# A graph network on one core: the opening of the kernel rebuilt

## The chip, the cores and the metric

The kernel runs on one core of one Trainium2 chip. A core has a matrix engine (TensorE, PE in the profile; its weight loads are PEld), a vector engine (VectorE, DVE), an activation engine (ScalarE, ACT), a general engine (GpSimd, POOL) and an engine that only issues transfers (SyncE, SP). Each engine works through its own list of instructions in order and waits for semaphores of the others. Transfers (DMA) are issued from SP, ACT or POOL and share 16 DMA engines. The metric is device time in microseconds (us) of one execution.

## What is computed

One layer on 64 graphs of 256 nodes with 256 features. The input is normalised per node and clipped at zero. Then come a convolution branch of width 1 and then 17 along the nodes, a message branch over an affinity matrix (with the given adjacency as a mask), and a gated recurrent unit that joins both; its result is added to the input.

```python
h = jnp.maximum(_layernorm(x, axis=-1), 0.0)
# inside the layer, on h:
h1 = relu(bn1(conv1(h)));  h2 = bn2(conv2(h1))       # conv2 has 17 taps, pad 8
x_conv = relu(h2 + h)
s = h @ w_se.T + b_se                                  # 3 features
A = exp(-dist(s)) * adj
x_nmp = A @ relu(h @ w_msg.T + b_msg)
gi = concat(x_conv, x_nmp) @ w_ih.T + b_ih
gh = h @ w_hh.T + b_hh
r, z = sigmoid(gi_r + gh_r), sigmoid(gi_z + gh_z)
out = x + (1 - z) * tanh(gi_n + r * gh_n) + z * h
```

All of it is float32.

## The kernel before

**Work and tiles.** Two graphs make a pair (`i`), four pairs a batch (`b`); there are 32 pairs and eight batches. The wide convolution is done in a transformed domain: each stretch of 16 nodes is transformed to 16 bins (`forward`, on DVE: `fft.odd` gives what bins 0 to 7 need, `fft.even` bins 8 to 15), every bin is multiplied with a transformed filter (`product`, on PE), and the products are transformed back (`branch_back`, `odd_back`, `q_back`, `p_back`, `join`, on DVE). Of each complex bin three real products are made, "kinds" 0, 1 and 2; bin 15 has two. That makes 47 products per batch, in the order of the list `TURNS`. `begin(m)` makes kind 0 of bins 2m and 2m+1, `complete(m)` the other kinds and evicts the result to `Yv` (odd bins) or `Yu`. Each product needs one transformed filter of 256 KB in one of nine slots `wb`, loaded by SP from the DRAM tensors `filt` (`load_kinds`), two new ones after each product that frees a slot.

**The opening.** The transformed filters are made once, at the start. The 17 taps of seven input channels are one group (`KG`); there are 18 full groups and a last one. `filters(p, m, g, eng)` multiplies group `g` of `taps` with the points of pass `m` (two matmuls of 256 columns), ACT evicts the result into one of eight buffers `fo` (the ring `evicted`), and a DMA from SP or POOL, in turn, stores it to `filt[m]`. Before, pass 0 has the bins 0 to 5, pass 1 the bins 6 to 11, pass 2 the bins 12 to 15, so 18, 18 and 11 columns per channel. The order is in `steps`: all passes of the first six groups, pass 0 of the others, the last group, then passes 1 and 2 of the others. `filter_steps(n)` plans the next `n`. The taps are loaded in three parts per half (`dc`), half 0 by SP and half 1 by ACT (lines 703 to 713).

Meanwhile the first four pairs are loaded, normalised (`stats`, `norm`: `bn_stats` and `bn_aggr` on DVE, a power on POOL for `rstd`, then the normalising on DVE), transposed on PE (`transpose_h`), passed through the first convolution (`conv1`, evicted with bn1's scale and shift) and combined into U and V (`split`). PE runs 35 matmuls on zeros first (`WARM`). The batch-norm vectors are loaded by POOL as rows and turned into columns by a transpose on PE (`columns`, `fold_bn`). Lines 1260 to 1293 are the opening: pairs with filter steps between them, `forward(0)` and `forward(1)`, filter steps, `load_kinds()`, `message(0)`, eight steps, `embed(0)`, four steps, `affinity(0)`, the remaining steps. `message` makes the messages and the 3-feature embedding, `embed` transposes the embedding, `affinity` makes exp(-dist) and masks it with the adjacency; `aggregate` multiplies with the messages.

**What sets the order.** The code above does not run as written. Every call goes through a `Recorder`, which notes for each instruction what it reads and writes. `emit()` then plans all instructions noted since the last `emit()`: it simulates the five engines and two DMA queues with estimated costs (line 334 on), and gives each engine, whenever it is free, the ready instruction with the earliest due time. Due times follow from the written order of PE's instructions. Instructions recorded while `nc.first` is set (the loads, the memsets before line 714) come first of all; `nc.behind = k` makes those that follow wait in the plan for instruction `k`. At most eight DMAs are planned in flight for SP and ACT together, eight for POOL. Before, the first `emit()` comes after the last filter step (line 1292), and the second, for all the rest, at the end. Tiles that only the opening needs (`taps`, `fo`, `points`) are in a pool that is closed there, and `Yv`, `w_x` and others take its place.

All recorded instructions carry line 371 in the profile; they are told apart by their tiles.

## Time and profile before

| | us |
|---|---|
| median of 6 runs | 1710.48 |
| lowest and highest run | 1705.96, 1714.1 |
| time of the profiled execution | 1705.96 |
| its span, first to last instruction | 1704.2 |
| PE busy in the span | 1667.5 |
| DVE busy | 1464.9 |
| ACT busy | 1043.0 |
| first matmul that is no warm-up | at 11.37 |
| first product | at 90.7 |

Times in the profile count from the start of the span. A row of the timeline gives start, length, engine, line, operation, the tiles written and read (`out<-in`), partitions and elements, how many instructions are merged in it, and in brackets the idle time of the engine before it with what ended that. PE busy time holds matmuls that run slowly and warm-ups, so a busy PE is not yet a useful one. The granted clock is a share of TensorE's full rate. Every float32 matmul is two records.

### The profile page before, as it was taken

What the parts mean: (1) busy time and instruction counts of PE and PEld (TensorE: products, weight loads), DVE (VectorE), ACT (ScalarE), POOL (GpSimd) and SP (SyncE); (2) the same over time, 40 slices, a digit from 0 to 9 for tenths busy, and PEclk for the clock granted to TensorE, in tenths of its full rate; (3) what the DMA queues carried; (4) which work ended last, traced back from release to release, by engine and by line L of the source; (5) the groups of instructions that cost most, each with busy time, mean ns of one, the idle gap of its engine ahead of it and who ended that gap; (6) DMA issues with size and microseconds to landing.
All of it is one profiled execution on the core that took longest, in us unless ns stands there. A gap on an engine that the chain in (4) does not pass through costs nothing.

```text
span 1704.2 us, 26232 instructions
## 1 busy us (share of the span) xinstructions
PE 1667.5 (98%) x9012; PEld 1422.0 (83%) x9012; DVE 1464.9 (86%) x3414; ACT 1043.0 (61%) x1951; POOL 222.2 (13%) x245
## 2 busy tenths in 40 slices
PE   8999999999999999999999999999999999999998
PEld 6788888888789788897888887898888978898886
DVE  7969899798897998799987998979988899879645
ACT  3545665577657756576565766567665776557453
POOL 4210021013110121101210021101211012000010
PEclk9999999999999999999999999999999999999999
DMA  9883565976469475783659745694656936484132
GB/s 231 268 266 111 123 129 109 279 161 131 110 170 265 92 139 111 202 237 76 135 113 260 180 90 119 132 288 121 124 114 187 250 90 121 100 240 128 23 61 51
DMA packets 326928, 261.47 MB, mean 153 GB/s; under 512 B 205011, under 2 KB 252399, under 8 KB 326794
## 3 DMA queue, kind: packets, MB, share of 16 engines
q1 hardware_dynamic: 294193, 214.32, 48.2%
q0 software_dynamic: 29520, 42.76, 13.3%
q10 hardware_dynamic: 3081, 2.71, 0.7%
q8 instruction: 71, 1.16, 0.3%
q14 instruction: 63, 0.52, 0.1%
HBM read 156.60 MB, written 43.78 MB: 118 GB/s over the span
## 4 chain that ended last, share of the span: by engine, by line
PE 82%; DVE 11%; DMA 4%; ACT 1%; issue 1%; ACTq 0%; SPq 0%; DVEq 0%
PE acc L371 56%; PE aux L371 26%; DVE V L371 2%; DVE T L371 2%; DMA wb<-filt 2%; DVE Yv L371 1%; DVE U L371 1%; DMA taps<-in_c_wT_dram 1%; DVE gn L371 1%; DVE tr L371 1%; DVE acc L371 1%; DVE wb L371 1%; DMA filt<-fo 1%; DVE msg L371 0%; DVE PT L371 0%
## 5 line engine op out<-in xcount | busy, mean ns | idle before, releaser
L371 PE MATMUL acc<-wb,w_ih 128*128 128x256 f32 x768 | 191.9, 379 | 0.0
L371 PEld LDWEIGHTS acc<-wb,w_ih 128*128 128x128 f32 x768 | 145.9, 190 | 19.8
L371 POOL DMA_DIRECT2D back<-in_x_dram x62 | 62.0, 1158 | 674.0 <-ACT back L371 568.9
L371 PE MATMUL aux<-wb,w_x 128*128 128x256 f32 x576 | 141.6, 383 | 0.6 <-ACT e L371 0.5
L371 DVE SCALAR_TENSOR_TENSOR V<-T,V 128x128 f32<-128x128 f32 (+2 forms) x448 | 141.3, 385 | 0.0
L371 POOL TENSOR_TENSOR rstd<-rstd,neg_half 128x4 f32<-128x4 f32 x32 | 74.7, 2335 | 505.6 <-DVE shift L371 302.8
L371 PE MATMUL acc<-wb,w_x 128*128 128x256 f32 x576 | 136.4, 381 | 1.8 <-DVE acc L371 1.8
L371 PEld LDWEIGHTS acc<-wb,w_x 128*128 128x128 f32 x576 | 108.1, 190 | 28.0 <-DVE acc L371 7.5
L371 PEld LDWEIGHTS aux<-wb,w_x 128*128 128x128 f32 x576 | 107.4, 190 | 20.8 <-issue 4.0
L371 PE MATMUL aux<-w_msg,hT 128*128 128x259 f32 x512 | 120.9, 381 | 0.0
L371 PE MATMUL acc<-V,wb 128*128 128x128 f32 x1024 | 120.4, 278 | 0.1
L371 PEld LDWEIGHTS acc<-V,wb 128*128 128x128 f32 x1024 | 118.2, 194 | 0.7 <-issue 0.3
L371 PEld LDWEIGHTS acc<-U,wb 128*128 128x128 f32 x1024 | 117.3, 192 | 0.9
L371 PE MATMUL acc<-U,wb 128*128 128x128 f32 x1024 | 117.9, 275 | 0.0
L371 PE MATMUL aux<-hT,w_c 128*128 128x512 f32 x224 | 107.9, 596 | 2.9 <-ACT e L371 2.7
L371 PE MATMUL acc<-wb,w_hh 128*128 128x256 f32 x384 | 110.0, 381 | 0.7 <-ACT acc L371 0.7
L371 PE MATMUL acc<-Yv,w_ih 128*128 128x256 f32 x380 | 108.0, 380 | 0.6 <-ACT Yv L371 0.6
L371 PEld LDWEIGHTS aux<-w_msg,hT 128*128 128x128 f32 x512 | 96.5, 190 | 14.4
L371 PE MATMUL acc<-hT,w_hh 128*128 128x256 f32 x380 | 104.5, 382 | 0.0
L371 PE MATMUL acc<-xnm,w_ih 128*128 128x256 f32 x380 | 103.9, 380 | 0.0
L371 PE MATMUL aux<-e,msg 128*128 128x256 f32 x448 | 103.1, 379 | 0.0
L371 ACT COPY back<-gn 128x1024 uint16<-128x1024 uint16 x62 | 80.5, 1351 | 32.3 <-DMA gn<-back 32.3
(190 smaller groups left out, 3787.4 us busy)
## 6 DMA issues: line engine op xcount, KB each, us to landing
wb<-filt SPq DMA_DIRECT2D x376, 256.0 KB
back<-in_x_dram POOLq DMA_DIRECT2D x62, 256.0 KB, 7.4
out_dram<-back POOLq DMA_DIRECT2D x62, 256.0 KB, 4.4
x<-in_x_dram SPq DMA_DIRECT2D x58, 256.0 KB
halves_d<-halves SPq DMA_DIRECT2D x28, 512.0 KB
adjh<-halves_d SPq DMA_DIRECT2D x112, 128.0 KB
hh<-halves SPq DMA_DIRECT2D x108, 128.0 KB
filt<-fo SPq DMA_DIRECT2D x18, 252.0 KB
```

The lines of the kernel that those rows point to most:

```text
L371: self.tasks.append(Task(engine, lambda: method(*args, **kw), cost, size, self.first))
```

## The change

- The loads of the opening are issued by SP: of ACT's there remain the first convolution's weights and the first points. The first points are loaded before x, bn2's vectors later, on POOL, behind the first power. The memsets of `h1` and `Z` are put behind it too.
- `WARM` is 21 instead of 35.
- The second pair's first statistics are planned behind the first pair's `rstd` addition, and its third behind the first pair's normalising. Two blocks of the first pair and all of pairs 1 to 3 are normalised on ACT (scale `rstd`, bias `h`, a new small DVE operation). One half of the first pair's relu and of its conv1 eviction go to ACT. bn1's columns and fold are planned behind the first two matmuls of conv1.
- The passes hold 16, 16 and 15 columns, cut from the list of turns (`PASSES`, `PLACE`), so the rows of `filt` are in the order of use.
- The `fo` buffers are pieces of `Yv`, which now lives from the start; the last pass is evicted onto the taps that it has just used.
- `forward` does the odd part of both halves first, then the even part of both.
- The last twelve filter steps, `embed(0)` and `affinity(0)` are written among `begin` and `complete` of bins 0 to 7, and the first `emit()` comes after `odd_back`.
- The adjacency of pairs 0 to 3 is loaded by `blocks` (rows in their order in memory); the copies in `embed` and `affinity` permute for it.

```diff
@@ passes and tiles
-    WARM = 35
+    WARM = 21
+    Yvt = keep("Yv", SL)
+    Yv = Slots(Yvt, GB * DC, L // 2, NW)
...
-            load_rows(adj_rows, adj, i, eng)
+            load_rows(adj_rows, adj, i, eng, blocks)
...
-    PASSES = [range(0, 6), range(6, 12), range(12, 16)]
+    TURNS = []
+    for m in range(0, BINS // 2, 2):
+        TURNS += [(n, 0) for n in range(2 * m, 2 * m + 4)]
+        for n in range(2 * m, 2 * m + 4, 2):
+            TURNS += [(k, kind) for kind in (1, 2) for k in (n, n + 1) if (k, kind) != (BINS - 1, 2)]
+    PASSES = [TURNS[a:a + 16] for a in range(0, len(TURNS), 16)]
+    PLACE = {t: (m, k) for m, p in enumerate(PASSES) for k, t in enumerate(p)}
-    evicted = Ring(stage.tile([P, W], FP, name=f"fo{k}") for k in range(8))
+    evicted = Ring(Yvt[:, k * W:(k + 1) * W] for k in range(8))
@@ loads
+    nc.scalar.dma_start(out=w_c1, in_=c1_wT.rearrange("(k p) o -> p k o", p=P))
     load_vectors("bn1", bn1, nc.gpsimd)
-    load_vectors("bn2", bn2 + [ih_b, hh_b], nc.gpsimd)
-    nc.scalar.dma_start(out=w_c1, in_=c1_wT.rearrange("(k p) o -> p k o", p=P))
+    load_points(0, nc.scalar)
     for j in range(PB):
         load_x(j)
-    load_points(0, nc.scalar)
-    for dc, eng in ((0, nc.sync), (1, nc.scalar)):
-        load_taps(dc, *PARTS[0], eng)
-        load_last_taps(dc, eng)
+    for dc in range(DC):
+        load_taps(dc, *PARTS[0], nc.sync)
+        load_last_taps(dc, nc.sync)
     for n in range(1, len(PASSES) + 1):
-        load_points(n, nc.scalar)
+        load_points(n, nc.sync)
     for part in PARTS[1:]:
-        load_taps(0, *part, nc.sync)
-        load_taps(1, *part, nc.scalar)
-    load_last_group(0, nc.sync)
-    load_last_group(1, nc.scalar)
+        for dc in range(DC):
+            load_taps(dc, *part, nc.sync)
+    for dc in range(DC):
+        load_last_group(dc, nc.sync)
     nc.first = None
-    nc.gpsimd.memset(Z, 0.0)
...
-    nc.gpsimd.memset(h1, 0.0)
@@ stats, norm
         for j in range(G * MC):
+            nc.behind = BEHIND.get((i, j))
             nc.vector.bn_stats(s[:, j, :], X[i][:, j, :])
+        nc.behind = None
...
         nc.vector.tensor_scalar(r, m[:, :, 1], LN_EPS, None, ALU.add)
+        if i < PB:
+            BEHIND[i + 1, 0] = nc.last["vector"]
...
     def norm(i):
         stats(i)
+        _, m, r, h = STATS[i]
+        if i < PB:
+            nc.vector.scalar_tensor_tensor(h, m[:, :, 0], -1.0, r, op0=ALU.mult, op1=ALU.mult)
         for j in range(G * MC):
-            nc.vector.tensor_scalar(X[i][:, j, :], X[i][:, j, :], STATS[i][1][:, j, 0:1], STATS[i][2][:, j:j + 1],
-                                    ALU.subtract, ALU.mult)
+            v = X[i][:, j, :]
+            if i == PB or (i == 0 and j < MC):
+                nc.vector.tensor_scalar(v, v, m[:, j, 0:1], r[:, j:j + 1], ALU.subtract, ALU.mult)
+            else:
+                nc.scalar.activation(v, v, AF.Identity, scale=r[:, j:j + 1], bias=h[:, j:j + 1])
+        if i == 0:
+            BEHIND[1, MC] = nc.last["vector"]
@@ transpose_h, conv1
-            if i == 0:
+            if i == 0 and dc == 0:
                 nc.vector.tensor_scalar(t, u, 0.0, None, ALU.max)
...
+            if i == o == 0:
+                nc.behind = nc.last["tensor"]
+                bn1 = columns("bn1")
+                nc.behind = None
+                S1.extend(fold_bn(bn1, "bn1"))
...
-            if i == 0:
+            if i == 0 and o == 0:
                 nc.vector.tensor_scalar(v, u, s1[:, o:o + 1], h1_shift[:, o:o + 1], ALU.mult, ALU.add)
@@ filters, load_kinds
-        t = evicted()
+        t = taps[:, g].rearrange("p c o -> p (c o)") if m == len(PASSES) - 1 else evicted()
...
-            m = n // len(PASSES[0])
-            nc.sync.dma_start(out=slots[WB[-1][0]], in_=filt[m][:, 3 * (n - PASSES[m][0]) + kind])
+            m, k = PLACE[n, kind]
+            nc.sync.dma_start(out=slots[WB[-1][0]], in_=filt[m][:, k])
@@ the opening
     norm(0)
-    bn1 = columns("bn1")
-    s1, h1_shift = fold_bn(bn1, "bn1")
+    power = nc.behind = nc.last["gpsimd"]
+    nc.gpsimd.memset(h1, 0.0)
+    nc.gpsimd.memset(Z, 0.0)
...
+    load_vectors("bn2", bn2 + [ih_b, hh_b], nc.gpsimd)
+    nc.behind = None
...
-    forward(0)
-    forward(1)
-    filter_steps(len(steps) - (FULL - FIRST) - 4)
+    for kind in (0, 1):
+        for k in range(2):
+            forward(k, (kind,))
+    THIRD = FULL - FIRST
+    filter_steps(len(steps) - THIRD - 8)
     pending.extend(TURNS)
     load_kinds()
     message(0)
     filter_steps(8)
-    embed(0)
-    filter_steps(4)
-    affinity(0)
-    filter_steps(len(steps))
-    nc.emit()
-    stage_ctx.close()
...
@@ the loop over batches
         complete(0)
-        if b > 0:
-            embed(i)
+        embed(i)
         complete(1)
         fft.branch_back(Yv, T, 0)
+        if b == 0:
+            filter_steps(THIRD // 2, False)
         begin(2)
+        affinity(i)
...
         begin(3)
+        if b == 0:
+            filter_steps(len(steps), False)
         complete(2)
         complete(3)
         if b == 0:
             norm(nxt)
         fft.branch_back(Yv, T, 2)
         fft.odd_back(Yv, T)
+        if b == 0:
+            nc.emit()
+            stage_ctx.close()
...
```

With `wide` false, `filter_steps` takes its PSUM banks from `aux` alone, since the products hold `acc`.

## The prediction

> **What bounds the kernel now.** I read the page first: busy shares, then the chain that ended last.
>
> ```profile
> span 1704.2 us, 26232 instructions
> PE 1667.5 (98%) x9012; PEld 1422.0 (83%) x9012; DVE 1464.9 (86%) x3414; ACT 1043.0 (61%) x1951; POOL 222.2 (13%) x245
> PE 82%; DVE 11%; DMA 4%; ACT 1%; issue 1%; ACTq 0%; SPq 0%; DVEq 0%
> ```
>
> PE is busy for 98% of the span and is 82% of the chain. The change removes no useful matmul (filter evaluation stays at 55 steps of four records), so it can only win time in which PE stands, runs warm-ups or runs slowly. I looked for that time in the PE rows of the timeline from 0 to 170 us (columns: start, length, what, idle before it).
>
> ```profile
> 1.84 9.69 PE L371 MATMUL aux<-e 128*128 128x128 f32 x70 [1.84 <-POOL e L371]
> 11.37 0.27 PE L371 MATMUL aux<-ident,x 128*128 128x128 f32 x1
> 13.55 3.70 PE L371 MATMUL acc<-hT,w_c 128*128 128x512 f32 x8 [0.67 <-DVE hT L371]
> 17.09 0.93 PE L371 MATMUL aux<-ident,T 128*128 128x128 f32 x7
> 19.69 1.10 PE L371 MATMUL aux<-taps,points 119*126 119x256 f32 x4 [1.68 <-DMA taps<-in_c_wT_dram]
> 67.03 1.13 PE L371 MATMUL acc<-taps,points 119*126 119x256 f32 x4 [1.22 <-ACT fo L371]
> 84.75 0.66 PE L371 MATMUL aux<-ident,e 128*128 128x128 f32 x4 [1.10 <-DVE e L371]
> 107.19 0.52 PE L371 MATMUL aux<-ident,z 128*128 128x128 f32 x2 [0.46 <-ACT z L371]
> 108.48 0.69 PE L371 MATMUL aux<-zT 9*128 9x256 f32 x2 [0.77 <-ACT zT L371]
> 109.57 0.69 PE L371 MATMUL aux<-zT 9*128 9x256 f32 x2 [0.39 <-ACT zT L371]
> 162.97 1.13 PE L371 MATMUL acc<-Yv,w_ih 128*128 128x256 f32 x4 [0.59 <-ACT Yv L371]
> ```
>
> Useful work starts at 11.37; after it the waits up to 165 us are 1 to 2 us each. The DVE rows and SP's rows of the same view tell why the start is late:
>
> ```profile
> 9.71 0.43 DVE L371 BATCH_NORM_STATS2 st<-T 128x6 f32<-128x256 f32 x1 [2.19 <-DMA T<-in_x_dram]
> 10.06 1.37 DVE L371 TENSOR_SCALAR x<-x,mv,rstd 128x256 f32<-128x256 f32 x4
> 9.33 10.49 SPq L371 DMA_DIRECT2D taps<-in_c_wT_dram x5
> ```
>
> The first pair's `rstd` was ready at 8.37 (POOL's power, 7.33 plus 1.04), but its normalising stood behind statistics of the second pair, which waited 2.19 for its rows. Last, the table of windows (busy time of PE, PEld, DVE, ACT, POOL; granted clock; DMA share; GB/s):
>
> ```profile
> 0.00:20.00 20.00, 15.68 (x96) 13.02 (x97) 12.55 (x48) 2.08 (x3) 14.09 (x29) 1.00 1.00 212
> 40.00:50.00 10.00, 10.00 (x48) 8.24 (x48) 9.95 (x36) 6.37 (x12) 3.59 (x6) 1.00 0.68 194
> 70.00:80.00 10.00, 10.00 (x49) 7.72 (x48) 9.98 (x33) 7.36 (x20) 2.66 (x5) 1.00 1.01 319
> 111.00:114.00 3.00, 3.00 (x17) 3.00 (x16) 2.89 (x6) 0.27 (x1) 0.00 (x0) 0.51 0.31 87
> 166.00:169.00 3.00, 3.00 (x8) 2.37 (x8) 2.78 (x7) 1.44 (x4) 0.38 (x1) 0.50 0.00 0
> ```
>
> DMA is full at the start and almost full around 75 us. Twice, after PE's waits at 106 to 110 and 162 to 165, the granted clock is halved, for about 3.4 us each: in the trace's records matmuls start 213 ns apart from 111.1 to 114.5 instead of 111, and 427 instead of 216 from 165.7 to 169.1. A spell costs half its length, 1.7.
>
> **The change, part by part** (gains positive).
>
> *First normalising.* The second pair's statistics now stand behind `rstd` and behind the first normalising, and vector loads and memsets on POOL behind the power. The aggregate ends at 6.38 as before; `rstd`'s addition 0.2, hand-over and power 1.25 (the row gives 1.04 plus 0.18 of wait), the shift 0.2: 8.05. Two blocks on DVE at 0.34 end at 8.75; two on ACT at 0.5 apart (the later rows `hh<-x,shift,rstd` last 0.59) end at 9.25. Eight transposes at 0.11 keep PE until 9.9; the first half of hT is evicted on DVE (0.65 per block), the other on ACT (0.60). conv1 starts at 10.4 instead of 13.55: +3.1. The 21 warm-ups end, by the old rows (16 records to 5.34, then 0.11 each for 26), at 8.2, so they hold nothing. bn1's transpose (0.13) and its fold (0.69 on POOL) move behind conv1's first half; DVE needs s1 only after it, at about 14. No cost; uncovered it would be about 1, the fold's chain.
>
> [...] From 8.2 to 10.4 PE would have only 0.9 us of transposes; before, 17.09 to 19.69 held 0.8 us of transposes in 2.6 us and the clock stayed at 1.00, so I take nothing. [...]
>
> *Loads on SyncE.* ACT issued five taps loads and the three later points loads; all go to SP behind the eight x loads. Before the first filter step SP and ACT must bring 256 KB of w_c1, 57 of points, 2048 of x, 2 x 336 and 2 x 126 of taps, 3.28 MB. At the window's 212 GB/s that is 15.5 us: landing at about 16.3 instead of 19.5. PE is ready for it at 10.4 + 3.4 (conv1) + 0.9 (transposes) = 14.7, so the wait is 1.6 against 1.68: +0.1. Bounds: no wait, +1.7; taps landing as late as before, -3.1. SP's remaining loads last until about 25 us; queued behind them are its first filter stores, which had to wait until 22.11 before as well, and eight eviction buffers cover that.
>
> *Norms of pairs 1 to 3 on ACT.* Twelve operations move from DVE (0.34) to ACT (0.5): 6 us more on ACT between 10 and 40 us, where its three windows of 10 us were busy for 0.60, 5.45 and 5.03. hT and h evictions queue behind them, and PE waits for hT. From 0 (ACT has room) to 2 (one 0.5 us block ahead of each of four hT): -0.6, nearer to the free side.
>
> *Filters in thirds of 16, 16, 15 columns, by turn.* A store of the first two thirds shrinks from 252 to 224 KB, of the last grows from 154 to 210. For 24 stores before the products that is 0.67 MB less, 2.4 us of DMA at 280 GB/s; but PE comes 3 us earlier. So the wait for an eviction buffer at 67 us (1.22) stays: 0, between +1.2 and -3. The last third's twelve steps evict onto taps and wait for no buffer.
>
> *Products among the last filters.* embed(0) and affinity(0) move between the products, where PE has other work: the wait of 1.10 at 84.75 goes, +1.1. Products start 12 filter steps (10.4 us) and 3.4 us of embed and affinity earlier, near 68 instead of 90.7, so DVE can begin the back transform in 95 to 115, where it idled (4.75 and 5.28 busy in the two windows of 10 us from 90). At embed(1) the waits are 0.46 + 0.77 + 0.39, with 1.7 of halved clock: 3.3. I expect half gone, +1.7 (0 to 3.3). At 158 to 169: 0.20 + 0.59, and 1.7: 2.5, released by ACT behind a chain of DVE; half, +1.2 (0 to 2.5).
>
> *New waits.* Products then start while stores run. Between the first wb load (about 60 us) and the last, DMA must move 12.3 MB of wb, 2.5 of last-third stores, 2.25 of GRU weights, 1.5 of adj and x: 18.5 MB, 66 us at 280 GB/s, done at 126. PE needs 73 us from 68 (47 products of 0.86, 12 steps of 0.86, and two each of messages at 3.66, aggregates near 3.6 and embeds with affinity at 3.4, some 22): done at 141. On average DMA leads, at the beginning hardly: of nine loads of 0.9 us only a few have landed at 68. I put in -1.5; bounds 0 and -10, the latter if none is ahead of the products (nine loads of 0.9 plus one landing of 2).
>
> *Adjacency by blocks, permuted copies, the Yv tile's place.* adj(0)'s two loads took SP 3.54 us and are used by affinity(0), which comes later now. The permuted copies write 128 and 512 columns with a stride; hT's relu with such a pattern lasts 0.60 as plain copies do (0.59): 0, at most -0.3. The first Yv evictions now wait for the stores of the buffers that they overwrite, ten steps back: 0; uncovered, one store's landing, 6 us, falls under the new waits.
>
> Sum: 3.1 + 0.1 - 0.6 + 0 + 1.1 + 1.7 + 1.2 - 1.5 = 5.1. The profiled execution took 1705.96; it would take 1700.9. It was the fastest of six, 4.5 under the median, so I forecast 1710.48 - 5.1 = 1705.4.
>
> **The rivals.**
> 1. *All waits go.* 3.1 + 1.7 + 1.2 + 1.1 + 3.3 + 2.5 = 12.9: 1697.6. For it: each is a wait with a named releaser that the change touches. Against: the order is written from estimated durations, and the same planner left these waits in the order before.
> 2. *DMA takes the gain.* Taps land late (-1.6 against the forecast), halved clock and waits at embed(1) remain (-1.7), and the first wb loads cost 3 (-1.5): 1710.2. For it: DMA share 1.00 in the first 20 us and 1.01 at 70 to 80. Against: 0.68 at 40 to 50.
> 3. *Slower: SP's order.* Six of the last third's stores are issued by SP, between wb loads. A store waits for its eviction, and the wb loads behind it wait too. In SP's waits (0 to 100 us) ACT's evictions held it 25.9 us in 16 times, 1.6 on average, 5.1 at most. Six by 1.6 is 9.6; nine loaded buffers cover 9 x 0.86 = 7.7. That is inside my -1.5. At 5.1 each it is 31 - 7.7 = 23 more, 1726. It decides against the change when the mean hold passes 3.2 us ((7.7 + 6.6 + 5.1)/6, 6.6 being the gains without new waits). Against it: a filter step waits for no product, so PE and ACT can run it early.
> 4. *It doesn't reach the end.* Later batches are planned anew from other states. Their starts differ already: PE busy in the 30 us windows from 290, 490 and 690 is 27.65, 28.53, 27.52, a spread of 1 per batch. Over seven batches some +-3. Filter rows now lie 32 KB apart in memory instead of 36; adjh loads with that pitch show packets of 1 KB in 46 ns, the shortest of that size, so I price it at nothing.
>
> **How the numbers follow.** What a measurement can tell from no change is about 0.3%, 5.1 us: below 1705.35 is faster. Forecast 0.46 (1701 to 1709; 0.27 of it faster, 0.19 same), rival 1 0.23 (faster), rival 2 0.15 (0.13 same, 0.02 slower), rival 3 0.16 (slower); rival 4 is the forecast's spread. Faster 0.50, same 0.32, slower 0.18. The range leaves out the best of rival 1 and most of rival 3: 1696 to 1714.
>
> **What would show it.** Right: conv1's first matmul near 10.4, first taps matmul before 17.5, no wait over 1 for `e` in the first batch, first product (Sv, wb) near 70, no granted clock of 0.5 at 106 to 120, wb waits of PE under 3 before 150. Wrong: a taps wait of over 3; PE waiting for wb in the product phase; new halved spells between 8 and 14 or among the products; ACT late with hT in 15 to 35; other waits in batches two to eight.

## The result, and the profile after

The changed kernel takes 1706.11 us (median of 34 runs, 1701.27 to 1712.42) against 1712.03 for the kernel before (77 runs, 1703.04 to 1723.45): a ratio of 0.9964, 95% interval 0.9955 to 0.9973. That is 0.36%, some 6 us, where 5.1 were predicted (1705.4 us, from the 1710.48 of the first six runs). The profiled executions are 1702.98 after and 1705.96 before, 3.0 apart.

The page's head after, first the span and the busy times, then the chain that ended last:

```profile
span 1701.2 us, 26181 instructions
PE 1666.9 (98%) x8984; PEld 1422.1 (84%) x8984; DVE 1457.9 (86%) x3401; ACT 1052.6 (62%) x1967; POOL 231.3 (14%) x245
PE 82%; DVE 12%; DMA 4%; ACT 1%; issue 1%; SPq 0%; DVEq 0%; ACTq 0%
```

PE is as busy as before and as large a share of the chain: the page does not show where 6 us went. The PE rows of the timeline do, the same stretch as before (start, length, what, idle before it):

```profile
1.85 7.52 PE L371 MATMUL aux<-e 128*128 128x128 f32 x42 [1.85 <-POOL e L371]
9.27 1.19 PE L371 MATMUL aux<-ident,x 128*128 128x128 f32 x8
11.16 1.99 PE L371 MATMUL acc<-hT,w_c 128*128 128x512 f32 x4 [0.70 <-DVE hT L371]
17.89 1.09 PE L371 MATMUL aux<-taps,points 119*112 119x256 f32 x4 [1.36 <-DMA taps<-in_c_wT_dram]
70.92 3.74 PE L371 MATMUL acc<-Sv,wb 128*128 128x128 f32 x32
116.95 4.73 PE L371 MATMUL acc<-U,wb 128*128 128x128 f32 x40 [1.43 <-DMA wb<-filt]
```

These and one wait of 0.2 are all the waits between 9 and 175 us, 3.7 in sum. PE's own table of waits over the same stretch before, then after (released by, us in total, times, longest):

```profile
PE aux L371 <- DMA taps<-in_c_wT_dram: 1.7, 1, 1.7
PE acc L371 <- ACT fo L371: 1.2, 1, 1.2
PE aux L371 <- ACT zT L371: 1.2, 2, 0.8
PE aux L371 <- DVE e L371: 1.1, 1, 1.1
PE acc L371 <- DVE hT L371: 0.7, 1, 0.7
PE acc L371 <- ACT Yv L371: 0.6, 1, 0.6
PE aux L371 <- ACT z L371: 0.5, 1, 0.5
PE aux L371 <- DVE msg L371: 0.2, 1, 0.2
```

```profile
PE acc L371 <- DMA wb<-filt: 1.4, 1, 1.4
PE aux L371 <- DMA taps<-in_c_wT_dram: 1.4, 1, 1.4
PE acc L371 <- DVE hT L371: 0.7, 1, 0.7
PE acc L371 <- DVE acc L371: 0.2, 1, 0.2
```

Every wait for `fo`, `e`, `zT`, `z` and `Yv` is gone, one for `wb` is new. What did not go is the halved clock (windows after: busy times of PE, PEld, DVE, ACT, POOL; granted clock; DMA share; GB/s):

```profile
90.00:100.00 10.00, 10.00 (x50) 8.24 (x49) 5.75 (x17) 5.10 (x10) 2.80 (x4) 0.83 0.60 180
140.00:150.00 10.00, 10.00 (x55) 9.43 (x55) 7.09 (x17) 6.01 (x14) 0.56 (x1) 0.83 0.19 52
```

By the trace's record of the granted clock these are two spells of 3.4 us, from 92.6 and 140.4, where before had two of 3.4, from 111.1 and 165.7 (1 - 0.83 of 10 us at half rate is 3.4 as well). They moved; their number and length are the same.

To see when the lead is made, I count every matmul by its columns, the warm-ups at nothing, and ask when PE has done so many us of useful work (1635.1 in all, in both kernels):

| useful work done, us | 5 | 40 | 60 | 80 | 100 | 120 | 140 | 160 | 250 | 1000 | 1550 |
|---|---|---|---|---|---|---|---|---|---|---|---|
| before, at | 17.7 | 55.2 | 77.2 | 100.2 | 125.1 | 145.8 | 169.6 | 189.8 | 281.0 | 1046.2 | 1607.5 |
| after, at | 15.7 | 52.7 | 73.4 | 97.3 | 119.9 | 143.6 | 163.8 | 183.9 | 276.0 | 1041.6 | 1604.7 |
| lead | 2.0 | 2.5 | 3.8 | 2.9 | 5.2 | 2.2 | 5.8 | 5.9 | 5.0 | 4.6 | 2.8 |

The dips at 80 and 120 are mostly the moved spells. From 140 us of work on the lead is 5 to 6. It is made in the opening and carried; the last two us of it are lost near the end, where the profiled execution after has a halved spell at 1570.6 that the one before has not. The start of the second batch's products, 297.7 after and 303.6 before, serves below as the mark of what the opening is worth.

### The profile page after: what moved, and what is told of

It reads as the page before. It is cut to its first block, busy times and chain, and to the rows that moved or that the text cites. A ratio compares the mean times of both kernels' runs of the same rounds, so it can differ in the third digit from the quotient of the medians.

```text
span 1701.2 us, 26181 instructions
## 1 busy us (share of the span) xinstructions
PE 1666.9 (98%) x8984; PEld 1422.1 (84%) x8984; DVE 1457.9 (86%) x3401; ACT 1052.6 (62%) x1967; POOL 231.3 (14%) x245
## 4 chain that ended last, share of the span: by engine, by line
PE 82%; DVE 12%; DMA 4%; ACT 1%; issue 1%; SPq 0%; DVEq 0%; ACTq 0%
PE acc L371 56%; PE aux L371 27%; DVE V L371 2%; DMA wb<-filt 2%; DVE T L371 2%; DVE U L371 2%; DVE gn L371 1%; DVE tr L371 1%; DVE acc L371 1%; DVE wb L371 1%; DMA taps<-in_c_wT_dram 1%; DVE PT L371 1%; SPq L371 0%; DMA hh<-halves 0%; DMA x<-in_x_dram 0%
## 5 line engine op out<-in xcount | busy, mean ns | idle before, releaser
L371 PEld LDWEIGHTS acc<-wb,w_ih 128*128 128x128 f32 x768 | 145.9, 190 | 19.8
L371 POOL TENSOR_TENSOR rstd<-rstd,neg_half 128x4 f32<-128x4 f32 x32 | 81.9, 2560 | 472.8 <-DVE shift L371 283.6
L371 PEld LDWEIGHTS aux<-wb,w_x 128*128 128x128 f32 x576 | 107.8, 190 | 19.9 <-issue 4.0
L371 DVE TENSOR_TENSOR T<-Yv 128x512 f32<-128x512 f32 (+1 forms) x80 | 42.5, 581 | 78.3 <-ACT Yv L371 77.8
```

What stands on the lines that cost most here:

```text
L371: self.tasks.append(Task(engine, lambda: method(*args, **kw), cost, size, self.first))
```

## The experiments

All times below are against the kernel before, run on the same chip: 12 executions of each kernel, 6 of early, taps_later and three_edits, 9 of warm10. "Second batch" is the start of its first product in the one profiled execution. No run takes out, each by itself, the order of the first normalising, the order inside `forward`, the adjacency by blocks or the eviction onto the taps.

| run | ratio to before, 95% | median, us | second batch |
|---|---|---|---|
| the change | 0.9964, 0.9955 to 0.9973 | 1706.11 | 297.7 |
| warm35 | 0.9962, 0.9948 to 0.9977 | 1705.89 | 299.2 |
| dvenorm | 0.9966, 0.9950 to 0.9983 | 1705.97 | 299.8 |
| twoq | 0.9999, 0.9981 to 1.0017 | 1713.99 | 305.1 |
| twoq_dve | 1.0022, 1.0007 to 1.0038 | 1718.57 | 312.6 |
| bins | 0.9993, 0.9977 to 1.0009 | 1712.36 | 303.7 |
| apart | 0.9989, 0.9972 to 1.0007 | 1710.59 | 293.7 |
| apart_two | 0.9972, 0.9956 to 0.9987 | 1708.70 | 300.8 |
| mem | 0.9964, 0.9947 to 0.9981 | 1707.58 | 298.7 |
| early | 0.9950, 0.9932 to 0.9968 | 1704.44 | 296.4 |
| taps_later | 0.9942, 0.9924 to 0.9960 | 1703.30 | 296.1 |
| three_edits | 0.9947, 0.9926 to 0.9967 | 1704.29 | 298.9 |
| warm10 | 0.9959, 0.9942 to 0.9975 | 1706.30 | 297.4 |

An interval is some 3 us to each side. Only those of twoq, twoq_dve and bins lie clear of the change's; apart's begins where the change's ends, and the others overlap it. For the others the rows of the trace speak, with the caution that the spells fall differently in every execution.

### The start: 35 warm-ups again

```diff
-    WARM = 21
+    WARM = 35
```

> The changed kernel with 35 warm-up matmuls again, nothing else. They end near 11.5 us, so the first useful transposes start 2.2 us later than in the changed kernel (9.27). Theory (an earlier start is worth its whole length at the end): the second batch's first product (297.7 in the changed kernel, 303.6 before) moves by 2.2 to 299.9, and the time is 2.2 us longer than the changed kernel's, ratio to before 0.9977. Rival (the landing of the taps sets the pace): the taps' wait of 1.36 at 17.89 absorbs 1.4 of it, only 0.8 is left, 298.5 and a ratio of 0.9969.

Useful work started at 12.51 and conv1 at 14.11, 2.95 later than in the change. But the taps had landed by the time PE came to them, so the wait of 1.36 went:

```profile
14.11 1.98 PE L371 MATMUL acc<-hT,w_c 128*128 128x512 f32 x4 [0.57 <-DVE hT L371]
19.31 1.03 PE L371 MATMUL aux<-taps,points 119*112 119x256 f32 x4
```

The second batch came 1.5 later (both executions lose the same time to a halved clock before it), and the time did not move by anything that it could show. In this pair of profiles an earlier start of PE is thus worth about half of what it gains at the first matmul: the rest is waited away for the taps.

### Norms of pairs 1 to 3 on DVE again

```diff
-        if i < PB:
+        if i == 0:
             nc.vector.scalar_tensor_tensor(h, ...)
-            if i == PB or (i == 0 and j < MC):
+            if i > 0 or j < MC:
                 nc.vector.tensor_scalar(v, v, m[:, j, 0:1], ...)
```

> The changed kernel with pairs 1 to 3 normalised on DVE as before (two blocks of the first pair stay on ACT). Theory of the prediction (ACT's extra 6 us delay hT, 0.6 us in all): the relu of the second pair's hT starts when its transposes end, not behind the third pair's normalising, and conv1 of the second pair starts up to 1 us earlier; second batch 297.1, ratio 0.9960. Rival (DVE, full from 30 us on, becomes the limit): transforms end 4 us later, first products wait, second batch 299 or later, ratio 0.9972 or more.

PE waited 2.24 for the taps instead of 1.36, and a halved spell followed (19.9 to 23.3), one more than the change has before its second batch. These two make 2.6 of delay, and a wait for `wb` shorter by 0.55 takes some of it back: that is the 2.1 by which the second batch is later, and nothing is left for the norms. The time stayed. So the rows show no difference that comes from where these norms run; one of less than 3 us would not show in the time.

### The loads on two queues again

```diff
-    for dc in range(DC):
-        load_taps(dc, *PARTS[0], nc.sync)
-        load_last_taps(dc, nc.sync)
+    for dc, eng in ((0, nc.sync), (1, nc.scalar)):
+        load_taps(dc, *PARTS[0], eng)
+        load_last_taps(dc, eng)
     for n in range(1, len(PASSES) + 1):
-        load_points(n, nc.sync)
+        load_points(n, nc.scalar)
...
```

(twoq; the later parts of the taps likewise, half 1 by ACT.)

> The changed kernel with the taps' and points' loads on SP and ACT again, in the same order otherwise (x and the first points first). Theory (bytes ahead of the taps set their landing, not the queue): the first complete filter step starts at 17.4 to 18.4 as in the changed kernel (17.89), the second batch's first product within 0.5 of 297.7, ratio 0.9964. Rival (two queues compete with x and hold the rows of the second pair): the taps' matmul at 19.7 as before, 1.8 more of waiting, 299.5 and a ratio of 0.9974.

The whole gain was gone, 6 us by the ratios. ACT's rows of the timeline show how; ACTq is its issuing of transfers:

```profile
11.74 0.60 ACT L371 ACTIVATE hT<-aux 128x512 f32<-128x512 f32 x1 [1.13 <-PE aux L371]
13.53 5.76 ACTq L371 DMA_DIRECT2D points<-points  x2
19.33 0.44 ACTq L371 DMA_DIRECT2D taps<-in_c_wT_dram  x1
19.82 2.08 ACT L371 ACTIVATE T<-T,shift,rstd 128x256 f32<-128x256 f32 x4 [7.49 <-DMA taps<-in_c_wT_dram]
```

Between 12.3 and 19.8 ACT computed nothing: issuing its loads took 6.2 us from 13.53, and by the profile a landing of taps ended its 7.49 us of idle time. The second pair's norms stand behind these loads in the same list (they started at 12.94 in the change). PE then waited 3.95 for them, and a halved spell followed:

```profile
20.48 2.16 PE L371 MATMUL aux<-ident,T 128*128 128x128 f32 x8 [3.95 <-ACT T L371]
```

The rival has a part in it too: DVE waited 1.50 for the second pair's rows at 7.59, ahead of the first pair's `rstd`, a wait that the change does not have, and conv1 started at 12.47, 1.3 later than in the change.

### Both: loads on two queues, norms on DVE

```diff
 # twoq and dvenorm together
```

> Both of 'twoq' and 'dvenorm': taps and points loaded by SP and ACT, pairs 1 to 3 normalised on DVE. In 'twoq' ACT's loads stood ahead of the second pair's normalising on ACT, which began at 19.82 instead of 12.94. Theory (the queue matters only because ACT now has early work behind its loads): without that work most of the loss goes, the second pair's transposes come at 16 to 17 instead of 20.48, second batch at 298 to 300, ratio 0.9965 to 0.9978. Rival (loads on two queues are slow by themselves): 303 or more, ratio 0.9990 or more.

If the loads hurt only because the norms came to stand behind them, this pair should have repaired it. It is the slowest kernel of the study; its rows on ACT and on PE:

```profile
19.38 8.87 ACTq L371 DMA_DIRECT2D taps<-in_c_wT_dram  x2
28.29 1.08 ACT L371 ACTIVATE hT<-aux 128x512 f32<-128x512 f32 x2 [16.25 <-DMA taps<-in_c_wT_dram]
```

```profile
28.95 3.78 PE L371 MATMUL acc<-hT,w_c 128*128 128x512 f32 x4 [8.73 <-ACT hT L371]
```

Now the second pair's relu (`hT`) stood behind the loads instead of its norms. The rival's numbers came out (303 or more, 0.9990 or more), but the rows name ACT's list for most of the loss, and in the kernel before, with the same loads on two queues, PE's longest wait at the start was 1.68. Work on ACT that the start needs early stood behind loads in ACT's list, with ACT idle for 7.49 us in twoq and for 16.25 here. This opening, in which ACT's work is due from 9 us on, depends on its not issuing them.

### Passes by bins again

```diff
-    PASSES = [TURNS[a:a + 16] for a in range(0, len(TURNS), 16)]
+    PASSES = [sorted(t for t in TURNS if t[0] // 6 == k) for k in range(3)]
```

> The changed kernel with the filters' passes by bins as before (18, 18 and 11 columns, bins 0 to 5, 6 to 11, 12 to 15) and all else as changed. Theory (the thirds by order of use give the DMA 0.67 MB less before the products and nothing else, 2.4 us of DMA, hidden or showing as a wait for an eviction buffer near 65 us): second batch within 0 to 1.5 of 297.7, ratio 0.9964 to 0.9972. Rival (order of use is what lets products start at 71): the first products wait for their filters, 299.5 or more, ratio 0.9975 or more.

Back to 18, 18 and 11 columns, with the products still among the last filters (the last group's filters keep the column numbers of the bins in turn and land in other places, so the products read other values; the number and size of its transfers are those of the edit). 5 us of the 6 went. The first products came 2.8 later, at 73.7: the stores of the two passes that they wait for are 252 KB again instead of 224, and the prediction had put that difference at 2.4 us of DMA, and its gain at 0. Then PE stood for 6.0 us:

```profile
111.94 2.07 PE L371 MATMUL acc<-V,wb 128*128 128x128 f32 x8 [5.99 <-DMA wb<-filt]
```

This is the 24th product. Its filter (bin 7, in the second pass) had long been stored; its load was issued at 100.4, behind five stores of the last pass, and landed 11.5 us later, when PE's wait ended. Two rows of SP's timeline and two of the DMA view for 100 to 112 us (queue, kind: packets, MB, share of the 16 engines' time) show between what it stood:

```profile
95.31 4.20 SPq L371 DMA_DIRECT2D filt<-taps  x5
100.39 2.03 SPq L371 DMA_DIRECT2D wb<-filt  x2
```

```profile
q0 software_dynamic: 530, 2.68, 61.6%
q1 hardware_dynamic: 910, 1.65, 38.4%
```

The queue `q0` is POOL's, and what it moves there is above all `w_ih` and `w_hh`, 2.25 MB, issued at 97.3 and 98.1. They take most of the DMA engines while PE lives on filters from `q1`. The same happens in the change, where the two weights were issued at 102.6 and 103.4 (the issue in bins, then in the change, and the change's DMA from 104 to 112 us):

```profile
97.31 0.79 POOL L371 DMA_DIRECT2D w_ih<-in_ih_wT_dram  x1
```

```profile
102.62 0.80 POOL L371 DMA_DIRECT2D w_ih<-in_ih_wT_dram  x1
```

```profile
q0 software_dynamic: 343, 1.93, 65.8%
q1 hardware_dynamic: 449, 0.82, 33.1%
```

In 8 us `q1` brought 0.82 MB, some three filters, where PE uses one in 0.9 us. Nine slots and the first aggregation (3.6 us at 109.0) carry PE over all of it but 1.43. With passes by bins the 24th load comes 6 us later than in the change (94.3 there), 3 us behind the weights instead of ahead of them, and the cover is short by 6. The two halved spells before the second batch are also twice as long as the change's (6.8 us from 108.9, partly inside the wait, and from 143.0). That is what the rows show of the 5 us. What made it so was not separated: the products start later, the weights leave 5.3 us earlier, and the plan mixes products and filter steps in another order from 84 us on. It was not the last third itself that PE waited for: that pass is used last in both cuts.

### Products apart from the filters again

```diff
-    filter_steps(len(steps) - THIRD - 8)
+    filter_steps(len(steps) - THIRD - 4)
     ...
     filter_steps(8)
+    embed(0)
+    filter_steps(4)
+    affinity(0)
+    filter_steps(len(steps))
+    nc.emit()
     for b in range(NB):
```

(apart; the calls inside the loop for b == 0 are taken out.)

> The changed kernel, but all filter steps, embed(0) and affinity(0) are planned and emitted before the first product, as before; loads, norms, thirds and buffers stay changed. Theory (planning the products among the last filters is worth the 2.5 us of the prediction's terms 1.1 + 1.7 + 1.2 - 1.5): the second batch's first product at 300.2, ratio 0.9979; a wait for e near 82 and waits at embed(1) followed by a halved clock come back. Rival (the halved spells only moved, from 111 and 165 to 92 and 140 us, and the gain is the start's alone): 297.7 to 298.5 and a ratio of 0.9964 to 0.9969.

This splits into two results. In the opening it was better: PE waited 0.4 in all from 60 to 175 us, and the second batch came at 293.7, 4.0 earlier than in the change; 1.7 of that is one halved spell fewer before it. The waits for `e`, `z` and `zT` that the theory expected did not come back. Over the run it was worse: 4.5 us by the medians, at no lower mean clock (0.9938 against 0.9931). The place of the first `emit()` is what the plan of all later batches starts from, and here it settled into another order. PE's order in batches 2 to 7 is another one in the two lists of instructions. Six batch lengths of the profiled execution are 202.4, 204.9, 205.7, 204.2, 205.3 and 201.8, against 200.8, 203.1, 201.2, 200.5, 201.4 and 198.7 in the change. They overstate the loss: this was the slowest of apart's twelve executions, five of its six batches hold a halved spell, at 1.7 us each, and one of the change's does.

So I split the two effects:

```diff
 # apart, and after the first batch's back transform:
         fft.odd_back(Yv, T)
+        if b == 0:
+            nc.emit()
         aggregate(i)
```

> As 'apart' (all filter steps, embed(0) and affinity(0) emitted before the first product), with one more emit after odd_back of the first batch, where the changed kernel has its own. By the lists of instructions PE's order in batches 3 to 8 is then that of the changed kernel and of the kernel before; in 'apart' it differs. Theory (merging products and filters costs 3 to 4 us in the opening, and 'apart' lost its lead by another order in the later batches): the second batch's first product again near 293.7, seven later batches of about 201 as in the changed kernel, ratio 0.9940 to 0.9950, faster than the changed kernel. Rival (merging is worth its gain by itself, later batches are slower for another reason): ratio 0.998 to 0.999 as 'apart'.

With a second plan boundary where the change has its first, the later batches were back at about 201, and 0.9972 stands beside 0.9964. Its profiled execution had taps landing late (a wait of 3.24, then a halved spell) and, with the two weights issued at 91.9 and 92.7, 3.7 us of waits for `wb` between 100 and 106, so its second batch at 300.8 is no clean measure. By the ratios merging is worth 1.4 us by itself, with some 3 to either side: small, and no more can be said of it.

### What is left in the opening

Memset of `h1` before the first power instead of behind it:

```diff
+    nc.gpsimd.memset(h1, 0.0)
     load_points(0, nc.scalar)
     ...
     power = nc.behind = nc.last["gpsimd"]
-    nc.gpsimd.memset(h1, 0.0)
```

> The changed kernel with the memset of h1 on POOL put before the first power (POOL is free from 4.1 to 7.0 us) instead of behind it. No engine's order of useful work changes. Theory (the memset, 8.01 to 9.06, holds the first normalising on DVE, which took 0.96 instead of 0.40): that instruction takes 0.40, conv1 starts at 10.6 instead of 11.16. At the end 0 to 0.5 us, since the taps' landing at 17.89 then costs a wait of 1.9 instead of 1.36. Rival (DVE is slow there for another reason, its neighbour on ACT): still 0.96.

DVE's first two normalisings, in the change and in mem:

```profile
8.25 1.28 DVE L371 TENSOR_SCALAR x<-x,mv,rstd 128x256 f32<-128x256 f32 x2
```

```profile
8.44 0.73 DVE L371 TENSOR_SCALAR x<-x,mv,rstd 128x256 f32<-128x256 f32 x2
```

The theory holds: without the memset beside them the two take 0.73, in three_edits too, and with it 1.28 in early as well; in bins, where the memset ended 0.39 after the first of them began, 0.85. conv1 came 0.35 earlier (10.81), which no single pair of profiles can show: with the same start as the change it lies between 10.68 (bins) and 11.49 (apart). The taps wait grew to 2.43, of which 0.71 is a later landing in this execution (18.60), and a halved spell followed. The time did not move.

All twelve steps of the last third before bins 4 and 5:

```diff
-            filter_steps(THIRD // 2, False)
+            filter_steps(THIRD, False)
         begin(2)
...
-        if b == 0:
-            filter_steps(len(steps), False)
```

> All twelve steps of the last third are planned before bins 4 and 5 begin, in place of six there and six after bins 6 and 7; the order of batches two to eight is unchanged. In the changed kernel PE waited 1.43 us for a filter (wb) at 115.5. Theory: that wait is what is left of the last third's late stores; it goes, the second batch's first product comes 1.4 us earlier (296.3 instead of 297.7) and the time falls by 0.08%, ratio 0.9956. Rival: with twelve steps ahead, the products come later and DVE, which transforms back, is late in their place: the wait goes and a wait for DVE or ACT of 1 to 2 us appears before 170, second batch at 297 to 299, ratio 0.9964 to 0.997.

The wait for `wb` is gone, and PE waits 0.4 in all from 60 to 175 us. The second batch came at 296.4; 296.3 was expected. No other wait over 0.2 took its place, and both kernels have two halved spells before the second batch. POOL issues the two weights behind its last filter store, now at 99.7 and 100.4, 3 us earlier, which fits the DMA view above. But an earlier issue is not enough by itself: in bins they left earlier still, and PE waited 6.0. No run moves the weights alone.

The first filter step behind the second pair's convolution:

```diff
+        if j == 1:
+            nc.behind = nc.last["tensor"]
-        filter_steps((1, 2, 3, 3)[j])
+        filter_steps((0, 3, 3, 3)[j])
+        nc.behind = None
```

> The first filter step is planned behind the second pair's first convolution, whose input is ready at about 17.4, so that PE needs no taps before 17.9, when they land. Theory (the landing of the taps set the pace of the start): the wait of 1.36 for taps goes, PE's useful work up to 30 us is 1.4 ahead of the changed kernel's, ratio 0.9956. Rival (the second pair's activations, ACT's norms and relu, are as late as the taps): PE waits about 1.3 for hT before 17.5 instead, and the gain is 0.5 at most, ratio 0.996 to 0.997.

PE did not wait for taps, and only 0.25 for `hT`. But in this profiled execution the clock was halved at the first convolution already:

```profile
9.31 1.19 PE L371 MATMUL aux<-ident,x 128*128 128x128 f32 x8 [1.07 <-DVE x L371]
11.21 3.30 PE L371 MATMUL acc<-hT,w_c 128*128 128x512 f32 x4 [0.70 <-DVE hT L371]
17.98 3.70 PE L371 MATMUL acc<-hT,w_c 128*128 128x512 f32 x8 [0.25 <-ACT hT L371]
```

```profile
11.70:15.30 3.60, 3.60 (x6) 1.35 (x5) 2.39 (x16) 2.15 (x5) 2.54 (x4) 0.53 1.18 155
```

So its useful work at 30 us was not ahead: the spell cost what the edit gained. That spell stands ahead of the place of the edit. Both kernels have two spells before the second batch (here from 11.7 and 93.6), so these cancel in the lead of 1.6 there, and the waits account for it: 1.36 for taps gone and 0.25 for `hT` new, 0.45 for `wb` instead of 1.43, 0.40 for ACT's eviction new. Some 1.1 of the lead is thus the edit's. Its median is the best of the study, but its interval overlaps that of the change: in the time it is promising, not shown.

The three together:

> The changed kernel with three edits together: the memset of h1 before the power, the first filter step behind the second pair's convolution, and the last third's twelve steps before bins 4 and 5. If the waits that are left in the opening are independent, 0.35 + 1.4 + 1.4 = 3.1 us come off: second batch's first product at 294.6, ratio 0.9945. If they only change places (for hT instead of taps, for DVE instead of wb, or a halved clock after a wait of over 2 us), it stays at 296 to 299 and the ratio at 0.996.

The start was clean (PE without taps wait, 1.1 us ahead of the change at 60 us of work), and the lead was gone by 140: there were waits of 1.1 for ACT's eviction of `acc` and of 0.85 for `wb`, and of the two spells one was as long as in the change and one twice as long, 6.8 us, 1.7 more of loss (windows of 6 us):

```profile
97.00:103.00 6.00, 6.00 (x37) 5.50 (x38) 1.15 (x2) 2.62 (x5) 2.44 (x4) 0.72 0.70 218
140.00:146.00 6.00, 6.00 (x33) 6.00 (x33) 3.54 (x7) 2.56 (x5) 0.55 (x1) 0.58 0.27 79
```

The second batch started at 298.9, 1.2 later than in the change: the start and the waits alone come out some 0.6 better than the change's, and the longer spell takes more than that. The small gains did not add up to 3.1. The median, 1704.29, cannot be told from early's or taps_later's.

### The clock at the start: 10 warm-ups

```diff
-    WARM = 21
+    WARM = 10
```

> The changed kernel with 10 warm-up matmuls (20 records) instead of 21 (42): by the row of the warm-ups (16 slow records to 5.34, then 0.11 each) they end at about 5.8, and PE has nothing until 9.3, 3.5 us. Prediction's assumption (idle time of that kind costs nothing): conv1's matmuls of pair 0 keep their 0.43 us each and the second batch's first product stays at 297.7, ratio 0.9964. [...]

```profile
1.84 4.64 PE L371 MATMUL aux<-e 128*128 128x128 f32 x20 [1.84 <-POOL e L371]
9.34 1.66 PE L371 MATMUL aux<-ident,x 128*128 128x128 f32 x8 [2.86 <-DVE x L371]
11.35 2.95 PE L371 MATMUL acc<-hT,w_c 128*128 128x512 f32 x4 [0.36 <-DVE hT L371]
```

After 2.86 us without work the first half of conv1 took 2.95 instead of 1.99, and the granted clock was 0.65 from 9 to 12 us and 0.78 from 12 to 15. conv1 ended 1.15 later than in the change. By 160 us of useful work the difference was 0.4 in its favour, and the time is the same.

## Why the prediction was right, and where its steps were off

The sum, by its terms. Measured is the difference of PE's rows, before to after:

| step | predicted | measured | from |
|---|---|---|---|
| first normalising: conv1 starts | +3.1 | +2.4 | 13.55, 11.16 |
| loads on SyncE: taps wait | +0.1 | +0.3 | 1.68, 1.36 |
| norms on ACT | -0.6 | 0 | no new wait for `hT` |
| thirds: wait for an eviction buffer | 0 | +1.2 | 1.22, none |
| wait for `e` | +1.1 | +1.1 | 1.10, none |
| embed(1): waits and half a spell | +1.7 | +1.6 | 0.46 + 0.77 + 0.39, none; spell stays |
| 158 to 169: likewise | +1.2 | +0.6 | 0.59 and 0.20, then 0.20; spell stays |
| new waits for `wb` | -1.5 | -1.4 | 1.43 at 116.95 |
| sum | 5.1 | 5.8 | lead at 140 to 160 us of work: 5.8, 5.9 |

**The forecast was right; part of that is luck.** The measured terms close the account, 5.8 of some 6. But only four of the eight came out within 0.3 of the forecast. The other four missed by -0.7, +0.6, +1.2 and -0.6, and most of that cancels in the sum.

**Mis-sized: the first normalising.** The step says "Two blocks on DVE at 0.34 end at 8.75". They ended at 9.53: 0.2 because the scale came at 8.25 and not 8.05, and the rest because the first of them ran beside POOL's memset of `h1`, which the change itself had moved there. I had counted what the move freed on POOL, not whom it would now run beside. mem shows it: the two take 0.73 together instead of 1.28.

**Mis-sized: the landing of the taps.** "landing at about 16.3" was 17.9, worked out from 3.28 MB at 212 GB/s. It hardly showed in the sum, because conv1 was late too. But it bounds the start, as warm35 shows: conv1 later by 2.95 cost only 1.5. That taps_later, which asks for the taps later, had no wait for them and lost only 0.25 to `hT` agrees.

**Mis-sized: the thirds, "the wait for an eviction buffer at 67 us (1.22) stays: 0".** It went. In the change the steps around 67 us follow one another without a wait, though PE came there 3.8 us earlier. Smaller stores are not what freed the buffers: in bins, with 252 KB again, PE has no such wait either. The other parts that could have done it (the last third evicted onto the taps, or SP's list without the two adjacency loads at that place) were not separated.

**Mis-sized: embed(1) and 158 to 169, in their parts.** I took half of waits and spells together; in fact all the waits went but 0.2, and none of the spells. The parts cancelled, by luck.

**Credited to the wrong part: the waits for `e`, `z` and `zT`.** The step "Products among the last filters" has "the wait of 1.10 at 84.75 goes, +1.1", since embed(0) and affinity(0) move between the products, and it expects half of the time lost at embed(1) to go because the products start earlier. The waits went. But apart plans embed(0), affinity(0) and all filters ahead of the products again, has its first product at 84.8, and has none of these waits either. So 2.7 of the sum's measured 5.8 did not need that part of the change; which other part removed them was not separated.

**What the sum missed altogether: the parts hold one another up.** It priced each part against the kernel before, and that came out for the total. Taken out of the changed kernel, they cost something else. Loads on SyncE was +0.1 in the sum; without it 6 us are lost. The sum asked only when the taps land, not what stands behind ACT's loads in ACT's own list once the change moves early work there. Thirds by turn was 0, on the ground that PE would come 3 us earlier to smaller stores; without it 5 us are lost. The "-1.5" for `wb` held in size, but for another reason, and that is luck. The step expected the shortage at the beginning ("of nine loads of 0.9 us only a few have landed at 68"), where PE did not wait at all, and then "On average DMA leads", an average over 66 us. The wait came 45 us later, in some 10 us in which the GRU's weights, 2.25 MB of the 18.5, come between the filters.

**The rivals.** Rival 1 (all waits go): nearly all the waits went, but not the spells, which were nearly half of its extra gain. Rival 2 (DMA takes the gain): taps late by 1.6, but the wait for them did not grow. Rival 3 (SP's order) was decided where I had said, by how long ACT's evictions of the last third hold SP. SP's waits from 55 to 130 us have

```profile
SPq L371 <- ACT taps L371: 8.3, 6, 1.9
```

six holds of 1.4 on average, against the 1.6 assumed and the 3.2 from which it would decide. Rival 4 (later batches planned anew) did not happen here: the order of PE's work in batches three to eight is the same in both kernels. That it can happen, apart shows.

**Its signs and two of its figures.** One sign of being wrong did come: halved spells among the products, at 92.6 and 140.4. They stand in place of the two of before and cost the same, so the sum did not feel them. One sign of being right failed: the first taps matmul that had to wait came at 17.89, not before 17.5. The first product "near 68" does not follow from the step's own figures (90.7 less 10.4, 3.4, the 2.6 of the start and 1.1 is about 73); it came at 70.92. Rival 3's 1726 should be 1727.

**Fewer warm-ups.** I took nothing for them, from a row of before. conv1 ran at full rate in ten of the eleven profiles with 21 warm-ups, the change's among them (granted clock 1.00 from 9 to 15 us). In taps_later's, with 1.07 and 0.70 us of idle time, it did not (0.50 from 12 to 15), and with 10 warm-ups and 2.86 us idle it did not either (0.65 from 9 to 12). No row of before shows how much idle time the start can stand; in the traces of all the runs 2.01 us of it or more within one stretch of 3.41 were followed by a halved clock in every case (last section). So "nothing" was the likely value, not a safe one. It cost no time in warm10, as the taps were late anyway.

## What to carry to other kernels

Before moving early work to an engine, look at what that engine issues: in twoq ACT stood idle for 7.49 us, until a landing of taps, with its work behind loads in its list, and no wait of the kernel before shows such a hold, as the engine has no work there. Only the length of its issue rows tells: ACT's two taps loads took 3.70 us from 13.33, where two others took 1.11 from 1.76. Price each part of a change twice, against the kernel before and by taking it out of the changed kernel; where the two differ, the parts need one another and must not be judged alone. And before gaining time at the start, find what the start runs into: here two us of earlier work met taps that landed when they landed. Where a wait goes, take out the part that was meant to remove it before crediting it.

## What the hardware showed that I had not expected

- **A memset on POOL stretched an operation on DVE.** The normalising that takes 0.40 alone (mem) took 0.96, ending at 9.21, 0.15 after the memset that ran beside it:

```profile
8.01 1.05 POOL L371 MEMSET h<- 128x1152 f32 x1
```

  In bins, where only 0.39 of the memset was left, it took 0.54 and ended 0.15 after it as well. Not every operation on DVE was held: the statistics at 7.85 (0.43) and the `shift` at 8.19 (0.15) ran beside the same memset and took as long as in mem without it (0.40 and 0.16). What sets that difference was not tried.
- **The spread of the runs follows the clock.** Within each kernel, over the 242 executions of this study, the time falls by some 1.5 us for each 0.001 that the mean granted clock is higher (correlation -0.85), about what one halved spell of 3.4 us costs, 1.7. Differences of a few us between kernels are of the size of two spells more or less, and where the spells fall changed with the order (111.1 and 165.7 before, 92.6 and 140.4 after).
- **The two queues did not share the DMA engines by need.** While `w_ih` and `w_hh` moved (the change, 104 to 112 us), POOL's queue had 1.93 MB in 343 packets to SP's 0.82 in 449: 2.35 to 1 by bytes, 0.76 to 1 by packets. In the trace the weights' packets are 6 KB (310 of the 343), the filters' 2 KB (401 of the 449). Whether the size of the packets makes the ratio was not tried.
- **A wait of over 2 us can cost more than itself.** After the taps waits of 2.43, 2.24 and 3.24 (mem, dvenorm, apart_two) and of 2.02 (twoq_dve) a halved spell followed; after 1.36, 1.62, 1.79 and 1.83 (the change, warm10, apart, early) none; after 2.22 (bins) none either. The traces' record of the granted clock tells 2.22 from 2.24. In every trace it changes only at whole multiples of 3.41 us after it first rises (in the change at 7.3; its first spells 25 and 39 stretches later). dvenorm's 2.24 lies within one such stretch; bins' 2.22 is cut by the end of one at 16.8, into 0.7 and 1.5. Over the whole of the fourteen traces there are 50 stretches in which PE had no matmul for 2.01 us or more, and every one was followed by a halved one; of the 101 with 1.0 to 1.9 us 12 were (1.70 in taps_later is one). Idle time is not the only cause: the spells at 92.6 and 140.4 came after stretches with none. What led to those was not tried.
- **The taps landed between 17.9 and 20.3 us** in the profiles of kernels that issue the same loads in the same order (the change 17.89, mem 18.60, apart 18.64, dvenorm 18.90, warm10 19.30, apart_two 20.30). What makes that difference was not tried.
